# The sum over states of two Mamba layers on TensorE: four 64x64 tiles, or two full 128x128 matmuls

## Chip, core and metric

One core of one Trainium2 chip. The metric is the device time of one execution in microseconds (us), the median over runs. The engines are TensorE (PE; its weight loads are shown apart as PEld), VectorE (DVE), ScalarE (ACT), GpSimdE (POOL) and SyncE (SP), whose queue issues the DMAs. All data is float32.

## What is computed

The input is x of shape (2, 256, 64, 64): two batches, 256 channels, 4096 positions. Layer 0 normalises it by groups, runs one Mamba block of 256 inner channels over the positions, and adds x. Layer 1 normalises by token and runs two Mamba blocks of 512 inner channels, one forward and one on the flipped sequence, and adds both. Then a mixture of eight experts (three matmuls each, weights from a softmax) runs on every token. The core of a Mamba block is:

```python
xz = x @ in_proj_w.T
xs, z = jnp.split(xz, 2, axis=-1)
xs = silu(conv4(xs) + conv_b)                    # 4 taps along the positions, by channel
dbc = xs @ x_proj_w.T                            # dt (16), B (16 states), C (16 states)
dt = softplus(dbc[..., :16] @ dt_proj_w.T + dt_proj_b)
h[t] = h[t-1] * exp(dt * A) + dt * xs * B[t]     # by channel and state
y = einsum('blds,bls->bld', h, C) + xs * D       # the sum over 16 states, and the skip
y = (y * silu(z)) @ out_proj_w.T
```

The change concerns the last line but one: the sum over states and the skip `xs * D`.

## The kernel before

**Tiling.** Channels lie on the 128 partitions, positions on the free axis, in chunks of 512. There are six jobs: layer 0 for batches 0 and 1, layer 1 forward for both, layer 1 backward for both. A job runs through its eight chunks in order, since the scan carries its state from chunk to chunk, so there are 48 steps (job, chunk). Two blocks of 128 channels make a *pair*; layer 0 has one pair, layer 1 two. Within a pair the 16 states are taken two at a time: a *quad* is two states times two channel blocks times 512 positions, and a pair has eight quads (n = 0 to 7). So a step of layer 0 has 8 quads and a step of layer 1 has 16, 640 in all.

**What a quad does.**

- POOL multiplies `dt * xc` (tile `xdt`, made once a pair at L516) by B into a tile `bq` (L518, `emit_b`). The `bq` pool has 6 buffers.
- ACT makes the decays `exp(dt * A)`, four instructions of 512 columns, into PSUM tiles `da` (L531, `emit_decay`; two buffers).
- DVE runs four scans (L541, `emit_scan`), one for each state and block. For n in 0, 2, 3, 5 the scan writes over `bq`; for the others it writes over `da`.
- The product with C is made by POOL in place in `bq` for n in 0, 2, 3, 5 (L566, `emit_times_c_quad`), after ACT has copied the last column of the states away for the next chunk (L561, `emit_carry`). For the other quads DVE makes it from `da` into `bq` (L552) and copies the last column itself (L555).
- PE adds the product of each state to the PSUM tile `y` (L576, `emit_sum`). This is the last reader of the `bq` buffer.

`y` holds both blocks of a pair in two PSUM banks and has one buffer. It is begun by the skip (L586, `emit_skip`), a matmul of `xc` with a diagonal matrix of D, and when all eight quads are added DVE multiplies it by the gate `sz` (L593, `emit_gate`).

**The sum before** does not use the array as one 128x128 matmul. `TILES` cuts it into four 64x64 tiles, (rows r, columns col, block j) = (0,0,0), (1,1,0), (0,1,1), (1,0,1). For each state, four matmuls add half a block each through a 64x64 piece of the identity:

```python
nc.tensor.matmul(
    y[i, jp][out_, r, :], ident[rows, rows], bq[g][rows, s, j, :],
```

Their results come out with the halves of the two blocks exchanged: `y`'s bank r holds, on columns col, the half r of block j. The host therefore puts the columns of W_in that make z, and the rows of W_out, in the same order (`summed`, `z_last`).

**The other work of a step.** The finished step's projection (L608 on PE, the residual added by DVE at L616) and the preparation of the next step (input projections L333, four-tap convolution as four matmuls with diagonal matrices L368, `dbc` L394, `dt` L415, the gates z, in layer 1 forward the normalisation of the next chunk L290 to L305) are laid between the quads: `Slots` keeps a list of pieces for each slot (one state of one quad) and queue, and the main loop runs the pieces of a slot around that state's own instructions. ACT copies the input projection to `xs` (L358) before the convolution can read it.

**What sets the order.** POOL's products are issued by a table written out by hand, where bN is the B product of quad N of the pair (8 to 10 being the next pair's) and cN the C product, and `POOL_C` gives for each quad on POOL the quad before which its sum is issued:

```python
POOL_C = {0: 2, 2: 4, 3: 5, 5: 7}
POOL_AT = {0: "b3", 1: "c0 b4 b5", 3: "c2 b6", 4: "c3 b7", 6: "c5 b8 b9", 7: "b10"}
```

From this program order a scheduler makes the final order of every engine; each engine then works through its own in order.

Of the kernel before, what the change touches and what calls it, by code (L numbers as in the profile page):

```python
# [35 lines left out]
P = 128  # L36
# [4 lines left out]
NS = 16  # L41
DTR = 16
QN = NS // 2


TILES = [(r, col, (col - r) % 2) for r, col in ((0, 0), (1, 1), (0, 1), (1, 0))]


POOL_C = {0: 2, 2: 4, 3: 5, 5: 7}
# [41 lines left out]
def hybrid_kernel(ctx: ExitStack, tc: tile.TileContext, a: dict, out: bass.AP):  # L91
# [7 lines left out]
    ident = const.tile([P, P], F32, name="ident")  # L99
# [39 lines left out]
    with ExitStack() as st:  # L139
# [92 lines left out]
        l0 = dict(W_in=a["l0_W_in"], W_x=a["l0_W_x"], W_dt=a["l0_W_dt"], W_out=a["l0_W_out"], vec=a["l0_vec"])  # L232
# [6 lines left out]
        cks = [{} for _ in steps]  # L239
# [249 lines left out]
        bq, bt, ct, da, y = {}, {}, {}, {}, {}  # L489
# [81 lines left out]
        def emit_sum(g, ss):  # L571
            i, jp, n = quads[g]
            for s in ss:
                for r, col, j in TILES:
                    rows, out_ = slice(64 * r, 64 * r + 64), slice(64 * col, 64 * col + 64)
                    nc.tensor.matmul(  # L576
                        y[i, jp][out_, r, :], ident[rows, rows], bq[g][rows, s, j, :],
                        start=False, stop=(n == QN - 1 and s == 1),
                    )

        def emit_skip(i, jp):
            job, _ = steps[i]
            y[i, jp] = ps_y.tile([P, 2, T], F32, tag="y", name=f"y_{i}_{jp}")
            for r, col, j in TILES:
                rows, out_ = slice(64 * r, 64 * r + 64), slice(64 * col, 64 * col + 64)
                nc.tensor.matmul(  # L586
                    y[i, jp][out_, r, :], job.w["d"][rows, 2 * jp + j, rows],
                    cks[i]["xc", jp][rows, j, :], start=True, stop=False,
                )

        def emit_gate(i, jp):
# [58 lines left out]
        for i, (job, c) in enumerate(steps):  # L650
# [33 lines left out]
            for q in range(np_ * QN):  # L684
                g = g0 + q
                _, jp, n = quads[g]
                for s in range(2):
# [9 lines left out]
                    if first == 3:  # L697
                        emit_skip(i, jp)
                    sl.run(slot, "pe")
                    if s == 0:  # L700
                        if g and (n - 1) % QN not in POOL_C:
                            emit_sum(g - 1, (1,))
                        for m, due in POOL_C.items():
                            if due == n:
                                emit_sum(g - n + m, (0, 1))
                    elif n not in POOL_C:
                        emit_sum(g, (0,))
# [37 lines left out]
        g = nq - 1  # L745
        emit_sum(g, (1,))
        i = len(steps) - 1
# [6 lines left out]
    with ExitStack() as st:  # L754
# [30 lines left out]
        of = mw.tile([P, 2, E, KC], F32, name="of")  # L785
# [75 lines left out]
        for i in range(NCH):  # L861
            xs, ns, wt = ready
            y = ps_o.tile([P, NB, KC, T], F32, tag="y", name=f"ym_{i}")
# [5 lines left out]
            for e in range(E):  # L869
# [6 lines left out]
                for b in range(NB):  # L876
                    nc.vector.tensor_tensor(h2[b], h2[b], over_channels(wb), ALU.mult)  # L877
                    for m in range(KC):
                        for k in range(KC):
                            nc.tensor.matmul(  # L880
                                y[:, b, m, :], we["Wo", e][:, k, m * P : (m + 1) * P], h2[b][:, k, :],
                                start=False, stop=(e == E - 1 and k == KC - 1),
# [3 lines left out]
            for b in range(NB):  # L886
                o = mk.tile([P, KC, T], F32, tag="o", name=f"o_{i}{b}")
# [88 lines left out]
```

## Time and profile before

| | |
|---|---|
| median of 8 runs | 7909.95 us (7907.12 to 7913.3) |
| the profiled execution, its own time | 7910.78 us |
| its span | 7908.9 us |
| PE busy | 5410.7 us |
| POOL busy | 4532.4 us |
| DVE busy | 4661.9 us |
| ACT busy | 3671.8 us |
| mean granted TensorE clock | 0.826 |
| the last sum over states | at 6138 us |

The profile's page gives the busy time of each engine, then the span in 40 slices of about 198 us with the busy share of each engine in tenths, the chain of work that ended last, and the costliest groups of instructions. A group's line reads: line of the code, engine, operation, output tile, input tiles, shapes, count; busy time and mean duration of one in ns; the idle time of the engine just before them and what ended most of it. The list of waits says which instruction waited for which, how long in all, how often, and the longest. A timeline's line gives start and length in us for a run of like instructions, with the idle time before it and its releaser in brackets. A matmul in float32 leaves two records, so 10240 records of L576 are 5120 matmuls: 640 quads, two states, four tiles.

### The profile page before, as it was taken

The numbers are of one execution on the slowest core, as the hardware profiler recorded it, in microseconds if no ns is written. First come the engines' busy times: TensorE is split into PE (matmuls) and PEld (weight loads), VectorE is DVE, ScalarE is ACT, GpSimd is POOL, SyncE is SP. The second block draws the span as 40 slices with busy tenths as digits, with TensorE's granted clock in tenths as the row PEclk, the third lists the DMA queues.
The fourth block names the chain that finished last, engine by engine and source line by source line (L and its number), as shares of the span: only waits on it lengthen the run. The fifth ranks groups of instructions, "written<-read, shape, count | busy, mean of one in ns | idle before, by whom it ended". The sixth has DMA issues, their size and how long they took to land.

```text
span 7908.9 us, 54386 instructions
## 1 busy us (share of the span) xinstructions
PE 5410.7 (68%) x18600; PEld 1940.8 (25%) x18600; DVE 4661.9 (59%) x4889; ACT 3671.8 (46%) x5392; POOL 4532.4 (57%) x1062
## 2 busy tenths in 40 slices
PE   6776676666666665665565555555555799999999
PEld 2222122121211221121121111111111344444444
DVE  7898776677667766676676667666767111111111
ACT  8885464544455444544444444445444222222222
POOL 6998777677677767776777677767778000000000
PEclk8888888788878887777777877777777899999999
DMA  5444343333333333333333333333333100000000
GB/s 188 160 158 154 138 149 129 115 129 130 114 120 126 128 117 118 115 138 119 115 120 121 115 118 118 127 113 112 123 120 115 46 11 11 11 11 11 11 0 11
DMA packets 254232, 806.99 MB, mean 102 GB/s; under 512 B 26362, under 2 KB 35330, under 8 KB 253954
## 3 DMA queue, kind: packets, MB, share of 16 engines
q1 hardware_dynamic: 253954, 803.53, 29.4%
q8 instruction: 145, 2.38, 0.1%
q14 instruction: 133, 1.09, 0.0%
HBM read 749.95 MB, written 53.48 MB: 102 GB/s over the span
## 4 chain that ended last, share of the span: by engine, by line
POOL 33%; issue 31%; PE 21%; DVE 7%; ACT 4%; DMA 1%; SPq 0%; POOLq 0%; DVEq 0%; ACTq 0%
POOL bq L518 25%; PE hp L846 12%; POOL bq L566 7%; PE ym L880 6%; DVE da L541 3%; POOL xdt L516 2%; DVE bq L541 2%; ACT da L531 1%; DVE bq L552 1%; PE wb L871 1%; DMA bc<-bcd 1%; PE lg L816 1%; PE var_m L132 1%; PE ym L866 0%; PE y L576 0%
## 5 line engine op out<-in xcount | busy, mean ns | idle before, releaser
L518 POOL TENSOR_TENSOR bq<-xdt,bc 128x2048 f32<-128x2048 f32 x640 | 2878.0, 4517 | 527.8 <-PE y L576 516.0
L531 ACT ACTIVATE da<-dt,w_a 128x512 f32<-128x512 f32 x2560 | 1754.1, 688 | 2373.5 <-DVE h_state L555 1602.5
L566 POOL TENSOR_TENSOR bq<-bq,bc 128x2048 f32<-128x2048 f32 x320 | 1446.2, 4522 | 863.9 <-ACT h_state L561 833.6
L541 DVE TENSOR_TENSOR_SCAN da<-da,h_state,bq 128x512 f32<-128x512 f32 x1120 | 1394.5, 1277 | 613.6 <-POOL bq L518 558.9
L541 DVE TENSOR_TENSOR_SCAN bq<-da,h_state,bq 128x512 f32<-128x512 f32 x1120 | 1357.0, 1265 | 602.2 <-POOL bq L518 491.2
L576 PE MATMUL y<-bq,ident 64*64 64x512 f32 x10240 | 1413.2, 647 | 134.7 <-POOL bq L566 69.5
L368 PE MATMUL conv<-xs,w_conv 128*128 128x512 f32 x1280 | 656.0, 660 | 393.7 <-ACT xs L358 393.7
L850 ACT ACTIVATE h<-hp,of,sc 128x512 f32<-128x512 f32 x512 | 398.0, 777 | 1025.3 <-PE hp L846 1025.3
L586 PE MATMUL y<-xc,w_d 64*64 64x512 f32 x640 | 194.4, 972 | 859.4 <-DVE sz L593 859.4
L552 DVE TENSOR_TENSOR bq<-da,bc 128x1024 f32<-128x1024 f32 x640 | 775.3, 1214 | 8.7
L877 DVE TENSOR_TENSOR h<-h,wbs 128x1024 f32<-128x1024 f32 x128 | 156.8, 1225 | 875.5 <-ACT h L850 875.5
L576 PEld LDWEIGHTS y<-bq,ident 64*64 64x64 f32 x10240 | 380.8, 144 | 1170.8 <-issue 932.1
L333 PE MATMUL z<-nx,w_in 128*128 128x512 f32 x640 | 409.4, 784 | 310.3 <-DVE sz L451 122.7
L394 PE MATMUL dbc<-xc,w_x 128*128 128x512 f32 x320 | 201.5, 760 | 461.6 <-DVE xc L382 397.5
L846 PE MATMUL hp<-n,W 128*128 128x512 f32 x1024 | 491.3, 634 | 0.0
L368 PEld LDWEIGHTS conv<-xs,w_conv 128*128 128x128 f32 x1280 | 259.2, 211 | 784.2 <-ACT xs L358 440.3
L880 PE MATMUL ym<-h,Wo 128*128 128x512 f32 x1024 | 449.9, 592 | 0.0
L846 PE MATMUL hp<-h,W 128*128 128x512 f32 x1024 | 449.9, 592 | 0.0
L333 PE MATMUL xs<-nx,w_in 128*128 128x512 f32 x640 | 328.5, 639 | 79.5 <-DVE sz L451 42.4
L608 PE MATMUL o<-sz,w_out 128*128 128x512 f32 x640 | 346.1, 678 | 19.1 <-DVE xc L382 17.9
L516 POOL TENSOR_TENSOR xdt<-dt,xc 128x1024 f32<-128x1024 f32 x80 | 188.3, 2353 | 204.1 <-DVE dt L430 187.0
L333 PEld LDWEIGHTS z<-nx,w_in 128*128 128x128 f32 x640 | 142.6, 242 | 553.1 <-DVE sz L451 156.7
(121 smaller groups left out, 4606.5 us busy)
## 6 DMA issues: line engine op xcount, KB each, us to landing
bc<-bcd SPq DMA_DIRECT2D x1280, 512.0 KB, 3.7
t_dram<-xr SPq DMA_DIRECT2D x48, 512.0 KB, 3.1
x<-t_dram SPq DMA_DIRECT2D x32, 512.0 KB, 5.7
xr<-t_dram SPq DMA_DIRECT2D x32, 512.0 KB, 5.3
x<-in_x SPq DMA_DIRECT2D x16, 512.0 KB, 6.1
xr<-in_x SPq DMA_DIRECT2D x16, 512.0 KB, 3.8
t_dram<-x SPq DMA_DIRECT2D x16, 512.0 KB, 3.4
n_dram<-nx SPq DMA_DIRECT2D x16, 512.0 KB, 5.9
```

The source lines that it names most:

```text
L333: nc.tensor.matmul(ps, job.w["in"][:, k, m * P : (m + 1) * P], rhs, start=(k == 0), stop=(k == KC - 1),)
L368: nc.tensor.matmul(v["ps"], w["conv"][:, j, k, :], job.xs[:, j, k : k + T], start=(k == 0), stop=(k == 3),)
L516: nc.gpsimd.tensor_tensor(ck["xdt", jp], ck["dt", jp], ck["xc", jp], ALU.mult)
L518: nc.gpsimd.tensor_tensor(bq[g], ck["xdt", jp].rearrange("p (o j) t -> p o j t", o=1).to_broadcast([P, 2, 2, T]), bt.pop(g).rearrange("p s ...
L531: nc.scalar.activation(da[g, s][:, j, :], cks[i]["dt", jp][:, j, :], AF.Exp, scale=steps[i][0].w["a"][:, 2 * jp + j, 2 * n + s : 2 * n + s ...
L541: nc.vector.tensor_tensor_scan(b if n in POOL_C else d[:, j, :], d[:, j, :], b, job.h[:, 2 * n + s, 2 * jp + j : 2 * jp + j + 1] if c else ...
L552: nc.vector.tensor_tensor(bq[g][:, s, :, :], d, ct[g][:, s : s + 1, :].to_broadcast([P, 2, T]), ALU.mult)
L566: nc.gpsimd.tensor_tensor(bq[g], bq[g], ct[g].rearrange("p s (o t) -> p s o t", o=1).to_broadcast([P, 2, 2, T]), ALU.mult,)
L576: nc.tensor.matmul(y[i, jp][out_, r, :], ident[rows, rows], bq[g][rows, s, j, :], start=False, stop=(n == QN - 1 and s == 1),)
L846: nc.tensor.matmul(ps, w[:, k, m * P : (m + 1) * P], x[:, k, :], start=(k == 0), stop=(k == KC - 1),)
L850: nc.scalar.activation(h[:, m, :], ps, AF.Relu, bias=of[:, l, e, m : m + 1], scale=sc[:, l, e, m : m + 1],)
L880: nc.tensor.matmul(y[:, b, m, :], we["Wo", e][:, k, m * P : (m + 1) * P], h2[b][:, k, :], start=False, stop=(e == E - 1 and k == KC - 1),)
```

## The change

`emit_sum` and `emit_skip` use the whole array: for each state two matmuls of 128x128, one for each block, instead of four of 64x64. The halves are no longer exchanged, so the host leaves z's columns and W_out's rows where they are. The tables for POOL are the same. Lines move up: L518 becomes L515, L541 L538, L566 L563, L576 L572, L586 L581, L608 L603, L616 L611.

```diff
-TILES = [(r, col, (col - r) % 2) for r, col in ((0, 0), (1, 1), (0, 1), (1, 0))]
...
         def emit_sum(g, ss):
             i, jp, n = quads[g]
             for s in ss:
-                for r, col, j in TILES:
-                    rows, out_ = slice(64 * r, 64 * r + 64), slice(64 * col, 64 * col + 64)
+                for j in range(2):
                     nc.tensor.matmul(
-                        y[i, jp][out_, r, :], ident[rows, rows], bq[g][rows, s, j, :],
-                        start=False, stop=(n == QN - 1 and s == 1),
+                        y[i, jp][:, j, :], ident, bq[g][:, s, j, :], start=False,
+                        stop=(n == QN - 1 and s == 1),
                     )
 
         def emit_skip(i, jp):
             job, _ = steps[i]
             y[i, jp] = ps_y.tile([P, 2, T], F32, tag="y", name=f"y_{i}_{jp}")
-            for r, col, j in TILES:
-                rows, out_ = slice(64 * r, 64 * r + 64), slice(64 * col, 64 * col + 64)
+            for j in range(2):
                 nc.tensor.matmul(
-                    y[i, jp][out_, r, :], job.w["d"][rows, 2 * jp + j, rows],
-                    cks[i]["xc", jp][rows, j, :], start=True, stop=False,
+                    y[i, jp][:, j, :], job.w["d"][:, 2 * jp + j, :], cks[i]["xc", jp][:, j, :],
+                    start=True, stop=False,
                 )
...
-    arrays["l0_W_in"] = z_last(l0["W_in"])
-    arrays["l0_W_out"] = l0["W_out"][summed(l0["W_out"].shape[0])]
+    for k in ("W_in", "W_out"):
+        arrays[f"l0_{k}"] = l0[k]
...
-        arrays[f"{d}_W_in"] = z_last(l1["in_proj_w"].T)
+        arrays[f"{d}_W_in"] = l1["in_proj_w"].T
...
-        arrays[f"{d}_W_out"] = l1["out_proj_w"].T[summed(l1["out_proj_w"].shape[1])]
+        arrays[f"{d}_W_out"] = l1["out_proj_w"].T
```

In the built program the number of instructions on the other engines stays, but for ACT's table loads (517 before, 531 after), and the scheduler's order moves in a few places: part of the sum of quad 2 stands before or behind the second convolution, in the backward steps the B product of the sixth quad goes ahead of the C product of the fourth on POOL, and DVE's gate (L593) and residual add (L616) stand one or two scans earlier in some steps.

## Prediction, made before the changed kernel was run

> **What bounds the kernel now.** I read the page from the top. Its first part gives the engines' busy time, its second their share in 40 slices:
>
> ```profile
> PE 5410.7 (68%) x18600; PEld 1940.8 (25%) x18600; DVE 4661.9 (59%) x4889; ACT 3671.8 (46%) x5392; POOL 4532.4 (57%) x1062
> ...
> PE   6776676666666665665565555555555799999999
> ...
> POOL 6998777677677767776777677767778000000000
> ...
> PEclk8888888788878887777777877777777899999999
> ```
>
> Two stages: 31 slices (to 6140 us) in which no engine is full, the scans, and nine with PE at 9, the experts. The change touches only the first. There the order of work bounds, a ring of POOL (`bq` products), VectorE (scans), PE (sums) and POOL again; the chain of waits has POOL at 33%, PE at 21%, and 31% no engine. Then the groups:
>
> ```profile
> L518 POOL TENSOR_TENSOR bq<-xdt,bc 128x2048 f32<-128x2048 f32 x640 | 2878.0, 4517 | 527.8 <-PE y L576 516.0
> ...
> L576 PE MATMUL y<-bq,ident 64*64 64x512 f32 x10240 | 1413.2, 647 | 134.7 <-POOL bq L566 69.5
> L368 PE MATMUL conv<-xs,w_conv 128*128 128x512 f32 x1280 | 656.0, 660 | 393.7 <-ACT xs L358 393.7
> ...
> L586 PE MATMUL y<-xc,w_d 64*64 64x512 f32 x640 | 194.4, 972 | 859.4 <-DVE sz L593 859.4
> ```
>
> and the waits (releaser; total, times, longest):
>
> ```profile
> PE y L586 <- DVE sz L593: 859.4, 66, 23.6
> ...
> POOL bq L566 <- ACT h_state L561: 833.6, 191, 11.0
> ...
> POOL bq L518 <- PE y L576: 516.0, 73, 14.7
> ...
> PE conv L368 <- ACT xs L358: 393.7, 44, 13.3
> ```
>
> The third matters: the sums of L576 are waited for by POOL, which needs a free `bq` buffer (73 times, 516 us), and otherwise by VectorE once, for 1.1 us. PE itself waits far longer, in a few long holes per step: that is the room for more work.
>
> **What a sum costs.** One place of a layer-1 step, PE's timeline (start, us, line, count of records):
>
> ```profile
> 3088.83 1.07 PE L576 MATMUL y<-bq,ident 64*64 64x512 f32 x2
> 3102.61 5.83 PE L368 MATMUL conv<-xs,w_conv 128*128 128x512 f32 x8 [12.71 <-ACT xs L358]
> 3108.37 1.94 PE L576 MATMUL y<-bq,ident 64*64 64x512 f32 x14
> 3110.24 1.98 PE L333 MATMUL xs<-nx,w_in 128*128 128x512 f32 x4
> 3112.16 1.09 PE L576 MATMUL y<-bq,ident 64*64 64x512 f32 x8
> 3113.18 3.70 PE L368 MATMUL conv<-xs,w_conv 128*128 128x512 f32 x8
> 3116.81 2.81 PE L576 MATMUL y<-bq,ident 64*64 64x512 f32 x24
> ```
>
> A matmul leaves two records. One state's sum is now four 64x64 tiles, 8 records; 24 records less 8 is 2.81 - 1.09 = 1.72 us, so a group takes 0.86 us, its four tiles side by side. A full matmul: conv's four less xs's two, 3.70 - 1.98 = 1.72, so 0.86 us each. Two full ones therefore take 1.72: **+0.86 us for each of 1280 groups, +1100 us of PE** (at the page's mean, 1413.2/1280 = 1.10 a group, it would be +1410). The skip (80 groups at 194.4/80 = 2.43 us, before two full ones at 0.86 warm to about 1.7 cold) changes by -0.7 to +1.0, in a hole. DMAs, SP's queue and the operations of the other engines keep their number; z's channels and W_out's rows only change places.
>
> Against the change's loss stands one drain: in this timeline a tiled run after a full one overlaps it by 0.06 us, like runs of one shape by 0.16 to 0.18, so about 0.1 us at each of some 20 changes of shape a step, 2 us a step, now gone. The Trainium skill, "TensorEngine Tiling (Array Packing)", Key Properties, says a change of tiling mode drains the engine; by it alone the change would gain in PE time.
>
> **Where it lands.** Two stretches, by window (length, busy PE, PEld, DVE, ACT, POOL, granted clock, DMA share, GB/s):
>
> ```profile
> 0.00:600.00 600.00, 422.65 (x1640) 132.17 (x1640) 506.04 (x554) 515.87 (x692) 503.66 (x123) 0.87 0.49 168
> ...
> 3000.00:3600.00 600.00, 373.14 (x1433) 120.16 (x1434) 418.69 (x436) 297.12 (x459) 426.32 (x101) 0.79 0.36 125
> ```
>
> A layer-1 step (161 us forward, 157 backward, gate to gate) has 32 groups, +27.5 us; its PE is 62% busy, so about 61 us idle, and it goes to about 80%. A layer-0 step (61.5 us in batch 0, 73 in batch 1) has 16 groups, +13.8, and goes from 70% to about 93% in batch 0. So nothing overflows on average; what counts is where a sum is waited for. I set each POOL wait for a buffer against the end of the sum that frees it:
>
> Layer 1: POOL's wait here is in the ring,
>
> ```profile
> 3110.41 4.51 POOL L518 TENSOR_TENSOR bq<-xdt,bc 128x2048 f32<-128x2048 f32 x1 [13.79 <-PE y L576]
> ```
>
> released 0.1 us after the sum of quad 2, which stands behind conv 1, which stands behind the xs copy. Now 14 records come after that conv (1.94 us); in the changed program's order two full matmuls come (1.88) in 14 forward steps, three (2.74) in the other 18: +0.8 there. The other buffers are free 1.5 us or more ahead of need (quads 1, 4, 11: 1.5, 3.1, 3.2), except quad 3 forward (0.3) and quads 0 and 14 backward (0.1).
>
> - *Layer 1 forward, 16 steps:* quad 3 late by 0.3 to 0.6 in some, gate and residual add one scan earlier: **+5** (0 to +50, if quads 1 and 4 use up their slack, 3 us a step).
> - *Layer 1 backward, 16 steps:* the order of POOL changes in 15: the `bq` product of a pair's sixth quad now goes ahead of the C product of its fourth. VectorE waits for it now:
>
> ```profile
> 4495.75 4.81 DVE L541 TENSOR_TENSOR_SCAN bq<-da,h_state,bq 128x512 f32<-128x512 f32 x4 [3.86 <-POOL bq L518]
> ```
>
> That goes: -3.9, less +1.0 (quad 0's buffer), +0.8 (above), +0.3 (projection) = -1.8; times 15 = -27. But 8.8 us are waited for POOL at the next quad, which may take it back, so I count half: **-14** (-60 to +15).
> - *Layer 0, batch 0, 8 steps,* the fullest place:
>
> ```profile
> 337.03 0.69 DVE L616 TENSOR_TENSOR xr<-o,xr 128x512 f32<-128x512 f32 x1 [3.57 <-PE o L608]
> ```
>
> VectorE waits for the projection, which stands behind two sums after a hole (3.7 us cold; four full ones, cold then warm, 5.7): +2.0 times 8 = 16; in 3 steps this add stands one or two scans earlier, about 2 us each, 6; 14 more table loads of 1.28 us on ScalarE (86% busy here), a third exposed, 6: **+28** (0 to +50).
> - *Layer 0, batch 1:* the ring runs through dbc, dt and xdt, sums lie beside it: **+3** (-16 to +16). The end (last sum, 0.9 before the last gate) and the 0.8 of two forward steps: **+2**.
>
> Sum 5 - 14 + 28 + 3 + 2 = **+24**. The profiled execution is 7910.78 us (span 7908.9, 1.9 around it), 0.8 over the median of 7909.95, so 7910.8 + 24 - 0.8 = 7934, **predicted 7934 us**, slower by 0.3%.
>
> **Rivals.**
> 1. *The cover gives way* (slower): PE's order is fixed, so a sum that is late holds all behind it. If the slacks of 1.5 to 3.2 us at quads 1, 4 and 11 are used up, each step waits some 3 us more: 32 x 3 = 96, and layer 0 by its upper end, 50: about 8055. For: layer 0 at 93%. Against: the holes of 12 us. It decides once a sum comes over 1.5 us late; fully exposed, +1100, 9010, would need PE without holes.
> 2. *Faster:* the swap of POOL's order holds in full, -3.9 x 15 = -59, and layer 0 loses only 10: about 7861. For: VectorE's wait of 3.86 is for exactly that product. Against: the wait after it. A second way to the same side is the clock: the conv after the hole takes 5.83 us, others 3.70, 2.1 more; if PE stayed warm there, -2.1 x 32 = -68. The Trainium skill, "TensorE: Matmul & The Clock Gate", Part 1, puts the drop at an idle window of about 3.4 us; by it the sums would have to shorten the hole of 12.7 below that. I reckon it shrinks to 7 to 9 (one step's sums ahead of it grow by 4 to 5), so the conv stays cold.
> 3. *Nothing on the path:* PE's holes take all, orders equal out: 7910 within 8.
>
> **Numbers.** Forecast 0.48 (own range 7900 to 7965; 0.16 of it below 7926), rival 1 0.20, rival 2 0.24, rival 3 0.08. About 0.2% (16 us) is what a measurement of this kernel can tell from no change. Faster 0.25 (rival 2 and a sliver), same 0.25, slower 0.50. The range leaves out a part of rivals 1 and 2: 7870 to 8040.
>
> **What would show it.** L576 with 5120 records of 128*128 and 2100 to 2800 us busy, PE at 80% or so to slice 31, the wait `POOL bq L518 <- PE y` near 516 (over 620 is rival 1); steps gate to gate: forward 161 within 0.5, backward 156 to 157, batch 0 of layer 0 near 65; the granted clock above 0.79 and the first conv still near 5.8. I am wrong if layer 1 forward grows over 2 us a step, if the sixth quad's scan still waits 3.9, or if that conv falls to 3.7.

## The result and the profile after

The changed kernel takes **7933.68 us** (median of 11 runs, 7930.15 to 7936.31), the kernel before 7909.24 (31 runs): ratio 1.0031, 95% interval 1.0023 to 1.0038. The forecast was 7934. The profiled execution has a span of 7929.8 us, 20.9 over the span before. The page, first two parts:

```profile
PE 6204.7 (78%) x13160; PEld 2659.6 (34%) x13160; DVE 4667.9 (59%) x4889; ACT 3692.7 (47%) x5406; POOL 4531.9 (57%) x1062
...
PE   7888777677777777777777777776777799999999
...
PEclk9999888888888888888888888888888899999999
```

PE has 794 us more to do, and the span grew by 21: almost all of it lies in what were holes (times in which PE stood idle). The groups and the waits that answer to those of before:

```profile
L572 PE MATMUL y<-bq,ident 128*128 128x512 f32 x5120 | 2380.1, 612 | 86.8 <-POOL bq L563 47.8
...
L365 PE MATMUL conv<-xs,w_conv 128*128 128x512 f32 x1280 | 653.9, 659 | 276.1 <-ACT xs L355 275.1
...
L581 PE MATMUL y<-xc,w_d 128*128 128x512 f32 x320 | 266.1, 958 | 541.2 <-DVE sz L588 541.2
```

```profile
POOL bq L515 <- PE y L572: 553.7, 66, 15.5
PE y L581 <- DVE sz L588: 541.2, 64, 14.8
...
PE conv L365 <- ACT xs L355: 275.1, 40, 9.7
```

PE's own waits shrank (skip 859 to 541 us, conv 394 to 275), which is where the work went; POOL's wait for a sum grew by 38 us only.

The start of each step's gate (L593, now L588) gives the time by stage, in us, and the loss by stage (one profiled execution of each kernel):

| stretch, gate to gate | before | after | difference |
|---|---|---|---|
| layer 0, batch 0 | 430.8 | 448.8 | +18.0 |
| layer 0, batch 1 | 515.3 | 517.2 | +1.9 |
| layer 1 forward, first step of batch 0, of batch 1 | 157.2, 153.1 | 163.8, 160.1 | +6.6, +7.0 |
| a middle step, forward (mean of 12) | 161.36 | 161.34 | 0.0 |
| layer 1 forward, last but one step of batch 1 | 155.8 | 160.2 | +4.4 |
| last step forward, first step backward | 161.2, 148.8 | 155.3, 158.8 | -6.0, +9.9 |
| a middle step, backward (mean of 11) | 157.11 | 155.28 | -1.8 |
| last backward step of batch 0, first of batch 1 | 161.2, 148.8 | 154.8, 159.0 | -6.5, +10.1 |
| last backward step but one of batch 1 | 154.6 | 149.9 | -4.7 |

Where a backward job begins, the step before it is some 6 us shorter and its first step 10 us longer, so each of the two places loses about 4. The 515.3 is not firm: in two runs below whose order is that of before in layer 0 (the swap alone and the filled hole) this stretch took 511.9, so the +1.9 may as well be +5.

### The profile page after: what moved, and what is told of

Its sections match the earlier page's. It is cut to its first block, busy times and chain, and to the rows that moved or that the text cites. A ratio compares the mean times of both kernels' runs of the same rounds, so it can differ in the third digit from the quotient of the medians.

```text
span 7929.8 us, 43494 instructions
## 1 busy us (share of the span) xinstructions
PE 6204.7 (78%) x13160; PEld 2659.6 (34%) x13160; DVE 4667.9 (59%) x4889; ACT 3692.7 (47%) x5406; POOL 4531.9 (57%) x1062
## 4 chain that ended last, share of the span: by engine, by line
issue 32%; POOL 31%; PE 23%; DVE 8%; ACT 3%; DMA 2%; SPq 0%; POOLq 0%; DVEq 0%; ACTq 0%
POOL bq L515 23%; PE hp L841 12%; POOL bq L563 7%; PE ym L875 6%; DVE da L538 3%; DVE bq L538 2%; POOL xdt L513 2%; PE y L572 1%; DVE bq L549 1%; ACT da L528 1%; PE wb L866 1%; PE lg L811 1%; PE var_m L129 1%; DMA t_dram<-xr 1%; DMA bc<-bcd 1%
## 5 line engine op out<-in xcount | busy, mean ns | idle before, releaser
L515 POOL TENSOR_TENSOR bq<-xdt,bc 128x2048 f32<-128x2048 f32 x640 | 2878.3, 4518 | 556.1 <-PE y L572 553.7
L572 PE MATMUL y<-bq,ident 128*128 128x512 f32 x5120 | 2380.1, 612 | 86.8 <-POOL bq L563 47.8
L563 POOL TENSOR_TENSOR bq<-bq,bc 128x2048 f32<-128x2048 f32 x320 | 1446.4, 4521 | 858.5 <-ACT h_state L558 855.6
L538 DVE TENSOR_TENSOR_SCAN da<-da,h_state,bq 128x512 f32<-128x512 f32 x1120 | 1397.6, 1278 | 603.8 <-POOL bq L515 553.9
L538 DVE TENSOR_TENSOR_SCAN bq<-da,h_state,bq 128x512 f32<-128x512 f32 x1120 | 1357.4, 1264 | 558.9 <-POOL bq L515 447.3
L572 PEld LDWEIGHTS y<-bq,ident 128*128 128x128 f32 x5120 | 1014.4, 199 | 1417.1 <-issue 1283.5
L581 PE MATMUL y<-xc,w_d 128*128 128x512 f32 x320 | 266.1, 958 | 541.2 <-DVE sz L588 541.2
L330 PE MATMUL z<-nx,w_in 128*128 128x512 f32 x640 | 369.3, 718 | 229.5 <-DVE sz L448 112.4
L330 PE MATMUL xs<-nx,w_in 128*128 128x512 f32 x640 | 307.1, 603 | 22.6 <-DVE sz L448 15.1
L581 PEld LDWEIGHTS y<-xc,w_d 128*128 128x128 f32 x320 | 85.0, 289 | 674.0 <-DVE sz L588 594.5
L603 PE MATMUL o<-sz,w_out 128*128 128x512 f32 x640 | 305.8, 613 | 2.1 <-DVE sz L448 1.3
```

The source lines that it names most:

```text
L330: nc.tensor.matmul(ps, job.w["in"][:, k, m * P : (m + 1) * P], rhs, start=(k == 0), stop=(k == KC - 1),)
L515: nc.gpsimd.tensor_tensor(bq[g], ck["xdt", jp].rearrange("p (o j) t -> p o j t", o=1).to_broadcast([P, 2, 2, T]), bt.pop(g).rearrange("p s ...
L538: nc.vector.tensor_tensor_scan(b if n in POOL_C else d[:, j, :], d[:, j, :], b, job.h[:, 2 * n + s, 2 * jp + j : 2 * jp + j + 1] if c else ...
L563: nc.gpsimd.tensor_tensor(bq[g], bq[g], ct[g].rearrange("p s (o t) -> p s o t", o=1).to_broadcast([P, 2, 2, T]), ALU.mult,)
L572: nc.tensor.matmul(y[i, jp][:, j, :], ident, bq[g][:, s, j, :], start=False, stop=(n == QN - 1 and s == 1),)
L581: nc.tensor.matmul(y[i, jp][:, j, :], job.w["d"][:, 2 * jp + j, :], cks[i]["xc", jp][:, j, :], start=True, stop=False,)
```

## Experiments

Each of these is timed beside the kernel before on the same chip. What was open after the result: whether these stage differences belong to the stages; and, since the scheduler laid out a new order for the changed kernel, how much of each is the longer sums and how much the order.

**One stage at a time.** A flag for each job chooses full matmuls or tiles in `emit_sum` and `emit_skip`, and the host leaves or exchanges the halves of that job's weights to match:

```diff
+FULL = (0,)          # e1: layer 0; (1,): layer 1 forward; (2,): layer 1 backward
...
+                if steps[i][0].full:
+                    for j in range(2):
+                        nc.tensor.matmul(y[i, jp][:, j, :], ident, bq[g][:, s, j, :], ...)
+                    continue
```

> Full matmuls in layer 0's jobs alone, tiles in the layer-1 jobs (their weights in the tiles' order). By the gates of the two traces (the time at which DVE's gate L593 of each step starts), the changed kernel is 18.4 us late at the end of layer 0's first batch and 20.7 us at the end of the second. Theory 1, the change costs by stage and the stages add: 7909 + 20 = 7929 us (7922 to 7936), and steps of layer 1 as before. Theory 2, the scheduler's new order of the whole program makes the differences, and a part of the change draws another order: anything within 30 us of before, with layer-1 steps that differ too.

Measured 7932.1 us, ratio 1.0027 (1.0017 to 1.0037): +20.5. The batch-0 stretch is 449.0, the backward steps are those of before.

> Full matmuls in the two forward jobs of layer 1 alone. In the changed kernel these 16 steps take 18 to 19 us more (6.6 and 7.0 of it in the first step of each batch, nothing in the other steps up to the last). Theory 1, stages add: 7909 + 18 = 7927 us (7920 to 7934), steps in the middle of a batch within 0.3 us of 161. Theory 2, orders: the two first steps keep their time, and the sum is near 7912. A third reading, that the 27 us of added PE work a step are exposed in part, would show in every middle step.

Measured 7932.0 us, ratio 1.0026 (1.0016 to 1.0035): +20.4. Middle steps stay between 160.6 and 162.5; the first step of each batch is up by 5.5 and 8.0.

> Full matmuls in the two backward jobs of layer 1 alone. In the changed kernel these steps take 1.8 us less each in the middle of a batch, about 18 to 20 us in all. Theory 1, stages add: 7909 - 19 = 7890 us (7882 to 7896), faster than both kernels, middle steps 154.3 and 156.4 in turn as in the changed kernel. Theory 2, orders: the gain needs what the scheduler does elsewhere, and the time is near 7909.

Measured 7895.4 us, ratio 0.9979 (0.9970 to 0.9988): -16.2, with middle steps that alternate between 154.3 and 156.3 as in the changed kernel. The three parts sum to 20.5 + 20.4 - 16.2 = +24.7; the whole change measured +24.4. **The totals add**, within intervals of some 8 us on each part. The gates do not all follow: in the profiled execution with full matmuls in the forward jobs alone (7939.8 us, 7.9 over its median) the 16 forward steps are 9.5 us longer and the 16 backward steps, still tiled, 14.4, of which 7.0 in the first; a part of what a job costs shows in the next one. So the change is a loss in two parts and a gain in a third.

**The swap of POOL's order.** One dependency for order only, in the kernel before (n counts from 0, so the fourth quad is n = 3):

```diff
+            if steps[i][0].flip and steps[i][1] and jp == 0 and n == 3 and what == "c":
+                behind(ci[g], bi[g + 2])
```

It puts the C product of the fourth quad behind the B product of the sixth. On PE, VectorE and ScalarE the order stayed that of before.

> The kernel before, tiles everywhere, with one thing of the changed kernel's order: in the backward steps but the first of each batch, POOL makes the B product of a pair's sixth quad ahead of the C product of the fourth (13 places; nothing else moves on PE, DVE or ACT). Theory 1, my sum: the wait of 3.9 us goes, and the 2.1 us that the longer sums give back in the changed kernel are not paid here: 13 x 3.9 = 51 us, 7858 us (7850 to 7870). Rival: the next wait for POOL (8.8 us) takes back about half whatever the sums are: 13 x 1.8 = 24, 7885 us. Rival: the swap is worth nothing here, 7909 us, and the backward gain comes from the matmuls.

Measured 7865.3 us, ratio 0.9941 (0.9928 to 0.9955): -46, 3.6 for each of the 13 swaps, inside the range of theory 1; middle backward steps take 153.67, 3.4 less. The wait shown in the prediction (VectorE at 4495.75, 3.86 us) is gone. POOL, then VectorE, at the same place of this kernel:

```profile
4469.89 4.53 POOL L533 TENSOR_TENSOR bq<-xdt,bc 128x2048 f32<-128x2048 f32 x1
4474.37 4.53 POOL L582 TENSOR_TENSOR bq<-bq,bc 128x2048 f32<-128x2048 f32 x1
4480.15 4.53 POOL L582 TENSOR_TENSOR bq<-bq,bc 128x2048 f32<-128x2048 f32 x1 [1.25 <-ACT h_state L577]
```

```profile
4474.99 4.80 DVE L557 TENSOR_TENSOR_SCAN bq<-da,h_state,bq 128x512 f32<-128x512 f32 x4
...
4489.19 4.82 DVE L557 TENSOR_TENSOR_SCAN da<-da,h_state,bq 128x512 f32<-128x512 f32 x4 [8.82 <-POOL bq L533]
```

The next wait is 8.82 us, as long as before (8.79): it took nothing back, for POOL's C product that stands behind it also came earlier (POOL had idled 5.2 us before it, now 1.25).

**The swap undone in the changed kernel** (the B products of the sixth and seventh quad issued later in the program, and the sixth's held behind the fourth's C product by the same kind of dependency; the other engines keep their order):

> The changed kernel with the one swap undone: in 14 backward steps POOL makes the C product of a pair's fourth quad ahead of the B product of the sixth, as before; PE and DVE keep the changed kernel's order. The swap alone took 3.4 us off a step of the tiled kernel. Theory 1, swap and longer sums add: 7934 + 14 x 3.4 = 7981 us (7972 to 7990), middle backward steps near 158.7. Rival: the swap has worth only where the sums are short, because the longer sums free the buffer late anyway: 7934 + 14 x 1.7 = 7958 us or less.

Measured 7992.7 us, ratio 1.0103 (1.0089 to 1.0116): 59 over the changed kernel, 4.2 for each of 14, just above the range. The 14 are the 13 of the change and the last step, which had this order before as well. The rival falls; the swap is worth more with longer sums, not less.

**Order and duration apart.** In each of the next two kernels every engine's instructions are chained, by dependencies for order only, in the order of the other kernel:

```diff
+    for engine, order in zip(("PE", "DVE", "Activation", "Pool", "SP"), ORDER):
+        mine = [i for i in traced if str(i.engine).endswith("." + engine)]
...
+                tc.add_manual_dep(mine[at], before.name, DependencyInfo(NoSync, DATA), reason="order")
```

> Tiled sums, with every engine's instructions chained in the changed kernel's order (each full matmul stands for two tiles). Against the changed kernel only the duration of the sums is another, against the kernel before only the order. Theory 1, order and duration both count: the order alone costs some 8 us in layer 0 and 14 at the first forward steps and gains 3.4 in each of 14 backward steps, 48: 7909 + 22 - 48 = 7883 us (7870 to 7895). Theory 2, the order alone makes the difference and the longer sums are wholly hidden: 7934 us. Theory 3, the duration alone: 7909 us.

Measured 7878.2 us, ratio 0.9960 (0.9948 to 0.9973).

> Full matmuls, with every engine's instructions chained in the order of before (a full matmul stands where the first of its two tiles stood, which puts three of four behind the second convolution in the forward steps). Theory 1: the longer sums cost some 14 us in layer 0, 1.7 us in each of 16 backward steps, 27, and up to 0.8 in each forward step, 13: 7909 + 54 = 7963 us (7945 to 7975). Theory 2, orders alone: 7909 us. Theory 3, duration alone: 7934 us.

Measured 7986.3 us, ratio 1.0095 (1.0082 to 1.0109). With the two kernels of the case that makes a square (medians, then steps gate to gate, us):

| | tiles | full matmuls | longer sums cost |
|---|---|---|---|
| order of before | 7909.4 | 7986.3 | +77 |
| order of after | 7878.2 | 7933.7 | +56 |
| *layer 0, batch 0*: order of before / after | 430.8 / 444.0 | 439.7 / 448.8 | +8.9 / +4.8 |
| *first forward steps*: before / after | 157.2, 153.1 / 164.1, 160.2 | 156.3, 154.6 / 163.8, 160.1 | about 0 |
| *middle forward step*: before / after | 161.36 / 160.44 | 162.28 / 161.34 | +0.9 / +0.9 |
| *middle backward step*: before / after | 157.11 / 153.67 | 159.52 / 155.28 | +2.4 / +1.6 |

**The new order gains 31 us, the longer sums cost 56, and the change is their difference.** Taken the other way round, the sums cost 77 in the old order and the new order then gains 53: the two are not independent, by 21 us. Theories 2 and 3 fall. In the old order the sums cost 77, more than the 54 expected and outside its range; one full matmul more behind the second convolution, which the rounding of tiles to full ones puts there, is in that number.

In layer 0 the price of the sums stands where the prediction put it. VectorE's wait for the projection in the same step, the changed kernel first, then its twin with tiles:

```profile
345.54 0.69 DVE L611 TENSOR_TENSOR xr<-o,xr 128x512 f32<-128x512 f32 x1 [4.68 <-PE o L603]
```

```profile
340.56 0.69 DVE L681 TENSOR_TENSOR xr<-o,xr 128x512 f32<-128x512 f32 x1 [3.33 <-PE o L673]
```

1.35 us here. This wait, summed over the eight projections of batch 0, is 8.2 us before, 16.7 with tiles in the new order, 13.2 with full matmuls in the old one, and 25.7 in the changed kernel. The eighth lies behind the stretch of the table; the seven inside it are 13.5 us more, of a stretch that is 18.0 longer.

**Why the first forward steps lose 7.** POOL there, in the kernel before and in the changed one:

```profile
2534.61 4.52 POOL L518 TENSOR_TENSOR bq<-xdt,bc 128x2048 f32<-128x2048 f32 x1 [4.61 <-PE y L576]
2539.70 4.52 POOL L566 TENSOR_TENSOR bq<-bq,bc 128x2048 f32<-128x2048 f32 x1 [0.58 <-ACT h_state L561]
```

```profile
2569.62 4.50 POOL L563 TENSOR_TENSOR bq<-bq,bc 128x2048 f32<-128x2048 f32 x1 [10.95 <-ACT h_state L558]
2574.09 8.96 POOL L515 TENSOR_TENSOR bq<-xdt,bc 128x2048 f32<-128x2048 f32 x2
```

Before, the B product of the seventh quad goes first; after, it waits behind the C product of the sixth, for which POOL stands idle 10.95 us. In all other forward steps but the last two *both* kernels have the second order. No run moves this order alone in the two first steps, but the loss goes with it: the kernels that have the second order there (the changed one, the forward jobs alone, the swap undone, tiles in the new order) lose 5 to 8 us in these steps, and those that have the first (layer 0 alone, the backward jobs alone, the swap alone, full matmuls in the old order) are within 1.5 us of before. That suggested a version beside the two, with the swap above and one more:

```diff
+            if steps[i][0].layer and what == "c":
+                if n == 5:
+                    behind(ci[g], bi[g + 1])
```

It puts the C product of the sixth quad behind the B product of the seventh, in both pairs.

> Tiles, the swap of the backward steps, and one more in all layer-1 steps: POOL makes the B product of a pair's seventh quad ahead of the C product of the sixth, as both kernels' scheduler left it in a few steps only. In a middle forward step VectorE waits 9.4 us for that B product in each pair, and the buffer is free about 8 us before POOL takes it. Theory 1, what VectorE waits for on POOL in a pair is on the path: 7909 - 46 (swap) - 8 x 32 at the second pairs alone = 7607 us, and down to 7400 with the first pairs. Rival: the ring through the second convolution sets the period, and the wait moves to it: 7865 us, like the swap alone.

Measured 7697.1 us, ratio 0.9730 (0.9717 to 0.9743), 168 below the swap alone. POOL in a middle forward step:

```profile
2014.79 4.52 POOL L536 TENSOR_TENSOR bq<-xdt,bc 128x2048 f32<-128x2048 f32 x1 [6.98 <-PE y L603]
2019.26 4.50 POOL L585 TENSOR_TENSOR bq<-bq,bc 128x2048 f32<-128x2048 f32 x1
```

The forward step went from 161.4 to 153.6, 7.8 of the 8 us expected; the backward step gained 3.4 beyond the swap, not 8, and no gain of the first pairs shows beside it, so the sum is short of the 7607 expected. The rival (7865) falls. Unlike the swap, this run does not isolate POOL: with the new dependencies the scheduler also moved instructions of VectorE and ScalarE, in well over a hundred places each.

**The ring through the second convolution.** The convolution of block 1 is put behind the whole sum of a pair's third quad (that sum is ready; the convolution, ahead of it on PE, waits for ScalarE):

```diff
+            if steps[i][0].layer and jp == 0 and n == 2 and i + 1 < len(steps):
+                behind(cks[i + 1]["conv", 1], mm)     # mm: the last matmul of this sum
```

> The kernel before with only the order on PE changed, the second convolution behind the third quad's sum in the layer-1 steps; POOL's order as before. Theory 1, the sum behind the convolution is what closes the ring, as the prediction read it (0.1 us of slack): VectorE's wait for the next product, 3.8 us, goes at least, and up to 10 us a step: 7909 - (120 to 320) = 7590 to 7790 us. Rival, another wait of the same length stands behind it: within 10 us of 7909.

Measured 7788.2 us, ratio 0.9849 (0.9833 to 0.9866): -121, 3.8 a step, the lower end: a middle forward step gains 4.2 us, a backward step 3.6. POOL's order is that of before; VectorE's and ScalarE's moved in some places here too, and in the next run.

> The tiled kernel with the new order on POOL of the run before, and one more order on PE: in the layer-1 steps the second convolution (which waits 5.6 to 12.7 us for ScalarE's xs copy) goes behind the whole sum of a pair's third quad, which is ready earlier and frees the buffer that POOL waits for. Theory 1, POOL's wait of 9.5 to 13.8 us for this buffer is on the ring: 4 to 9 us a step over 32 steps, 7697 - (130 to 290) = 7410 to 7570 us. Rival, the ring then runs through the convolution and its readers (dbc waits 12.8 us for xc): 7690 us.

Measured **7605.3 us**, ratio 0.9616 (0.9602 to 0.9630): faster than both kernels, by 304 us against the kernel before, but 92 us beyond the run with POOL's order alone, less than the 130 expected. Alone the same order gave 121, so 29 of it had been taken by the first.

> The same orders with full matmuls everywhere: what the longer sums cost once the ring has less slack. Theory 1, they cost about what they cost in the changed kernel's order, 56 us (7934 less the 7878 of tiles in that order): the time of the tiled twin plus 40 to 80 us. Rival, PE becomes the bound in layer 1 as its holes close (1100 us of added work, 140 us a step): the twin plus 150 us or more, and slower against it by 2%.

Measured 7674.7 us, ratio 0.9703 (0.9688 to 0.9717): 69 us over its tiled twin, within the 40 to 80 of theory 1, with PE 81% busy, so PE does not become the bound here. This pair was not chained, and the order of POOL, VectorE and ScalarE differs between the two, so the 69 is length and order together.

**The clock.** The prediction gave the second way to a faster kernel as the clock: the convolution behind the hole runs cold. The kernel before, its order chained, with zero matmuls that add nothing to the sum in that hole:

```diff
+                        for _ in range(10 if job.flip else 12):
+                            warm.append(nc.tensor.matmul(
+                                y[i - 1, 0][:, 1, :], zeros, cks[i - 1]["xc", 0][:, 0, :],
+                                start=False, stop=False,
+                            ).ins)
```

> The kernel before, every engine chained in its own order, with PE's hole before the second convolution of the layer-1 steps filled: 12 (forward) or 10 (backward) matmuls of a zero matrix with xc, added into the open sum, which they leave as it is; 0.86 us each, in 30 steps. In the trace of before this convolution takes 5.1 to 6.75 us after a hole of 10 to 13, and 3.6 to 3.7 everywhere else. Theory 1, the granted clock falls in the hole and the ring pays for it: filled, the convolution takes 3.6, 1.9 us less on average, 30 x 1.9 = 57, 7909 - 57 = 7852 us (7843 to 7865). Rival 1: the convolution is slow for another reason (its wait, the change of shape), 7909 us. Rival 2: the hole is needed, and filling it makes the convolution late: above 7909 us.

Measured 7895.8 us, ratio 0.9983 (0.9974 to 0.9992): -13, between theory 1 and rival 1. PE in a backward step, then two windows of it (columns as in the prediction; the granted clock is the third number from the end):

```profile
4492.07 8.75 PE L425 MATMUL y<-xc,zeros 128*128 128x512 f32 x20
4500.75 1.07 PE L648 MATMUL y<-bq,ident 64*64 64x512 f32 x2
4504.52 5.09 PE L431 MATMUL conv<-xs,w_conv 128*128 128x512 f32 x8 [2.70 <-ACT xs L413]
```

```profile
4500.75:4504.50 3.75, 1.07 (x3) 0.18 (x2) 3.38 (x5) 3.65 (x6) 0.00 (x0) 0.93 0.50 164
4504.50:4506.50 2.00, 1.98 (x3) 0.95 (x4) 2.00 (x3) 0.00 (x0) 0.00 (x0) 0.50 0.04 8
```

The hole left over is 2.70 us, and the clock still falls to 0.50. Of the 30 filled holes, the 8 that came out at 1.2 to 2.1 us left the convolution at 3.70 us, and the 22 of 2.5 to 3.1 left it at 5.1 to 5.4. In the full-matmul kernel with the new orders that hole is 1.6 us or less, and this convolution takes 3.70 in all 30 steps (there the third convolution is the cold one, 5.4 to 6.8 us behind holes of 4.1 to 4.3):

```profile
1949.14 3.70 PE L370 MATMUL conv<-xs,w_conv 128*128 128x512 f32 x8 [1.57 <-ACT xs L360]
```

So the convolution is slow because of the clock, and rival 1 falls as to its cause; rival 2 falls too. Seven forward steps are 1.3 to 2.9 us shorter than before, all others within 0.8; the two warm backward convolutions, in the first steps of their batches, shortened nothing. For the other 22 the filling was too short. A fuller one was not tried, so what a warm convolution is worth in every step stays open.

## Why the prediction was right, and where it was right by luck

**The bound and the cover: right.** Holes on PE took nearly all of the added work. The price of a sum came out at 2380.1/2560 = 0.93 us for a full matmul against the forecast 0.86. A group of two takes 1.86 against 1.10 for its tiles, 0.76 more, and PE's busy time on the sums is up by 967 us, less than the 1100 to 1410 forecast, whose lower end took the tiles at their warm price too. The granted clock went from 0.826 to 0.880, and PE's other work took some 245 us less. The skip rose by (266.1 - 194.4)/80 = 0.9 us, inside the bounds.

**Layer 0, batch 0: +28 forecast, +18 measured.** The mechanism (VectorE's residual add behind the sums) is the measured one, but the sums' part, put at 2.0 us in each of 8 steps, sums to 4.8 to 8.9 by the square; the order's part, put at 12 (moved adds and table loads), is 9 to 13. The term was mis-sized by charging every step: five of the eight projections do not wait for PE at all in the kernel before (the others 2.3 to 3.6 us), and what comes late there is partly hidden. Batch 1: +3 forecast, +1.9 measured, or about +5 against the shorter stretch named under the table.

**Layer 1 forward: the middle steps right, the first steps missed.** Forecast +5 and 2; measured about 0 in the middle steps, +6.6 and +7.0 in the first step of each batch and +4.4 in the last but one, 17.6 in all up to there. The first steps go with an order on POOL that I had read for the backward steps and not for these; the +4.4 was not followed up. The square shows that the 0 is itself a sum: +0.9 from the sums, -0.9 from the order.

**Layer 1 backward: -14 forecast, about -17 measured** (from the gate before the last forward step on; -16.2 with the backward jobs alone). The step "-3.9 less 2.1 = -1.8" comes out to a tenth, but of terms that are each half a microsecond off: the swap gives -3.4, the sums +1.6, together -1.8 a middle step. "I count half, because the next wait may take it back" is wrong: the swap alone kept 3.4 of 3.86. The order also changes in 13 steps, not in 15. The full -1.8 in 15 steps would have given -27; measured are -20 in the eleven middle steps, about +8 where the two backward jobs begin (+9.9 and +10.1 in the first steps, less what the steps before them gain), and -5 at the end. With tiles in the new order the first steps are already 7.3 and 7.4 longer, so most of that is the order; what in the order does it stays open.

**What the sum is worth.** Three misses came out near zero: by the gates layer 0 was forecast 11 too high, layer 1 forward 13 too low, and the backward part, by the halving and the starts, 3 too high. The total of 7934 is closer than its terms deserve; the terms that stand are the price of a sum, its place behind the convolution, and the swap.

**The rivals.** The cover did not give way: POOL's wait for sums stayed at 554 us, below the 620 set for it. Rival 2's swap is real, -46 alone, but the change brought the longer sums with it. Its clock did not come: the hole shrank from 10 to 13 us to 6.7 to 9.7, as reckoned, and the convolution stayed at 5.2 to 6.75, as in this row of the changed kernel:

```profile
3127.51 1.88 PE L572 MATMUL y<-bq,ident 128*128 128x512 f32 x4
3138.20 5.36 PE L365 MATMUL conv<-xs,w_conv 128*128 128x512 f32 x8 [8.81 <-ACT xs L355]
3143.40 1.88 PE L572 MATMUL y<-bq,ident 128*128 128x512 f32 x4
```

The drain that the Trainium skill, "TensorEngine Tiling (Array Packing)", Key Properties, names for a change of mode agrees with the rows: a convolution takes 3.70 us behind a tiled sum, 3.60 behind a full matmul, 0.1 us. It is too small to turn the change.

## What to carry to other kernels

When an edit changes the length of an instruction under a scheduler, price the order and the length apart: here they were -31 and +56 (or +77 and -53, taken in the other turn), and chaining every engine in the other kernel's order measured each. Look for who waits for the lengthened work, not for how busy its engine is: 967 us of added PE work cost 56 to 77. And where an engine with a fixed order stands idle for an operand while ready work that others wait for stands behind it, move that work ahead: three such orders, two on POOL and one on PE, were worth 304 us together with what the scheduler moved beside them, twelve times the change itself.

## What the runs showed of the hardware

**The clock goes by the busy share of a window, not by the length of a gap.** The Trainium skill, "TensorE: Matmul & The Clock Gate", Part 1, ties the drop to an idle window of about 3.4 us. In the 14 traces the granted clock is 1.00 or 0.50 and changes only at multiples of 3.413 us from its first record. Until the last gate these traces hold 16253 such windows at full clock, and 3360 of them were followed by 0.50: every one in which PE was busy for less than 40.8%, and none above 52%. So much less than an idle window is enough here. With the hole filled, gaps of 2.5 to 3.1 us left a window 19 to 38% busy, and the convolution took 5.1 to 5.4 us (22 cases); gaps of 1.2 to 2.1 us left none under 49%, and it took 3.70 (8 cases). The length of the gap alone does not decide. Here are two convolutions, each with two windows of 3.41 us (the number behind the length is PE's busy time, the third from the end the granted clock): a gap of 2.11 us, parted between two windows, leaves the clock up (hole filled), and a gap of 1.90 us that lies in one brings it down (the order on PE alone).

```profile
2607.86 3.70 PE L431 MATMUL conv<-xs,w_conv 128*128 128x512 f32 x8 [2.11 <-ACT xs L413]
2606.13:2609.55 3.42, 1.69 (x4) 0.86 (x5) 3.29 (x5) 1.68 (x3) 0.00 (x0) 1.00 0.32 119
2609.55:2612.96 3.41, 3.41 (x19) 1.07 (x17) 3.34 (x5) 2.07 (x3) 0.00 (x0) 1.00 0.00 0
```

```profile
2129.70 5.40 PE L370 MATMUL conv<-xs,w_conv 128*128 128x512 f32 x8 [1.90 <-ACT xs L360]
2127.59:2131.00 3.41, 1.51 (x7) 0.67 (x4) 2.14 (x3) 3.38 (x7) 1.18 (x1) 1.00 0.28 115
2131.00:2134.42 3.42, 3.42 (x5) 1.35 (x4) 0.00 (x0) 0.06 (x1) 3.33 (x1) 0.50 0.00 0
```

In the experts seven windows of each trace were followed by 0.50 although PE was busy throughout; why stays open.

**A cold stretch has a length that depends on its phase.** In the changed kernel the same convolution takes 5.24 and 6.58 us in turn in the backward steps, and those steps take 154.3 and 156.3 us in turn; with tiles and the swap it takes 5.46 in every middle step, and each of these takes 153.6. So 1.34 of the 2.0 us between neighbouring steps of the changed kernel goes with the place of this convolution against the clock's windows, not with its work.

**The backward steps come in whole windows.** Their middle steps settle at 157.0 us before, 153.6 with the swap, 150.2 with the new order on POOL and 146.8 with the order on PE as well: 46, 45, 44 and 43 times 3.413 us, each to 0.02 us. Two neighbouring steps of the changed kernel take 310.6 us together, 91 windows. So each of these gains of 3.4 us is one window, also where the wait that went was 3.86 us long, and the +1.6 for the longer sums is about half a window a step. That the clock sets the length of these steps is the likely reading, for a cold convolution lies on their ring; no run moves the windows, so it is not shown. It does mean that a gain measured here need not be the length of the wait that was taken away.
